# Softmax shifts and residuals of the last units, moved from GpSimd to VectorE

## The chip, the cores and the metric

The kernel runs on one core of one Trainium2 chip. A core has five engines with a queue of instructions each: TensorE (PE in the profile, its weight loads PEld), VectorE (DVE), ScalarE (ACT), GpSimd (POOL) and SyncE (SP), which here only issues DMAs. An engine takes its instructions in the order in which they are written; engines wait for each other by semaphores. The metric is the device time of one execution in microseconds (us). The kernel before takes 2047.81 us, the median of four runs.

## The reference, cut to what matters

Four graph layers work on `x`, 32 graphs of 512 nodes with 64 features, and share one adjacency matrix of 512 x 512. Each layer first normalizes its input and applies a relu, and its result is added to its input. Layers 0 to 2 are done before the part that this document is on. Layer 3 is graph attention with eight heads of width 128, and then one more attention to bring the result back to 64 features:

```python
def gat_layer(x, graph, W, b):
    h = x @ W
    s = jnp.einsum('bnd,bmd->bnm', h, h) * graph
    s = jnp.where(s == 0.0, NEG_INF, s)
    a = jax.nn.softmax(s, axis=2)
    return jnp.einsum('bnm,bmd->bnd', a, h) + b
heads = jax.vmap(lambda W, b: gat_layer(flow_x, graph, W, b))(Wh, bh)
x = jax.nn.leaky_relu(cat, negative_slope=0.01)
out = gat_layer(x, graph, W_out, b_out)
return jax.nn.leaky_relu(out, negative_slope=0.01)
# layer 3 of the stack: x = x + that
```

A softmax subtracts the largest score of a row before the exponential. The kernel has this subtraction as an operation of its own, called `shift`. The last sum, `x +`, is called the residual.

## The kernel before, in words

Layer 3 is cut into 144 units. A unit is a pair of attention matrices of 512 x 512: two graphs of one pair of heads (`Heads`, 128 units), or the second attention of two graphs (`Out`, 16 units). The list `flow` holds them in order; the last eight of the list are all `Out` units. In this document units are numbered from 0, so the last is 143. The function `period(t)` (L737) is called for t from -10 to 149 and writes out, in a fixed order, one step for each of several units that are at different stages: `unit(lag)` is unit t - lag, or nothing where there is none. TensorE, VectorE, ScalarE, GpSimd and SyncE all keep the order written there.

The scores of a unit are kept in four row blocks r = 0 to 3 of 128 rows, each a tile `p_att` of 128 x 1024 numbers of 4 bytes for the two matrices. Around the change, a unit u goes through these steps; the period in which it does is given as u + lag:

- lag 0: `scores` (L383, TensorE) and `maxima` (L395, VectorE) make each block and its largest values; `spread_out` and `spread_in` (L402, L410, SyncE) send these out and bring them back as a broadcast tile `topb` by DMA.
- lag 1: `shift(r, engine)` (L414 to L420) subtracts `topb` from block r. It is one operation of 128 x 1024 (L416), but two halves of 128 x 512 for r = 0 (L420). `exps(r)` (L429, ScalarE) takes the exponential, for r = 1 and 3 into PSUM (`e_ps`); `join(r)` (L432, VectorE) adds block r and block r - 1. `make_v` (L629 to L633) makes the right-hand sides.
- lag 2: `totals` (L450, TensorE, L456, ScalarE) and `totals_out` (L461, DMA to `parts`) make the sums of rows, `values` (L438, TensorE) the product with the features, `recips` (L467, L470, VectorE) the reciprocals, which `recips_out` (L474) sends out.
- lag 3: `recips_in` (L481) brings the reciprocals back as a broadcast tile `recb`, and `normalize` (L487, VectorE) multiplies by it.
- lag 4, `Out` units: `bias` (L660, ScalarE), `back` (L670 transposes on TensorE, L675 on ScalarE) and `back_dve` (L678, VectorE, the leaky relu).
- lag 5, `Out` units: `back_pool` (L684) adds the residual, in two operations of 128 x 256, one for each graph.
- lag 6, `Out` units: `store` (L691, SyncE), one DMA for each graph.

In every period but t = 1 all four shifts are GpSimd's. In t = 1, when nothing else runs yet, they are VectorE's, in the order 0, 2, 1, 3, at one place of the period: behind `normalize` of lag 3 and the maxima, and ahead of `back`, `back_dve`, `values`, `recips` and `join`. The residuals are all GpSimd's. At t = 145 `any_zero` (L695 to L720) works out a flag, which every engine reads at the end (L1839) to skip a general form of the kernel that isn't needed with these inputs.

Of the kernel before, what the change touches and what calls it, by code (L numbers as in the profile page):

```python
# [22 lines left out]
def fast_form(  # L23
# [25 lines left out]
    nc = tc.nc  # L49
# [276 lines left out]
    class Pair:  # L326
# [42 lines left out]
        def back_dve(self):  # L369
            pass  # L370

        def back_pool(self):
            pass

        def store(self):
# [224 lines left out]
    class Out(Pair):  # L600
# [78 lines left out]
                self.y, self.ps, -1.0, self.w, op0=OP.add, op1=OP.max  # L679
            )  # L680

        def back_pool(self):
            for k in range(2):
                nc.gpsimd.tensor_tensor(  # L684
                    self.y[:, :, k], self.y[:, :, k],
                    xs[self.b // G][:, self.b % G + k], OP.add,
                )
# [7 lines left out]
    def any_zero():  # L695

        def across(src, rows, name):
            ps = ps_m.tile([P, P], F32, name=name, tag="m")
            n = src.shape[0]
            nc.tensor.transpose(ps[:rows, :n], src, ident[:n, :n])  # L700
            return ps[:rows, :n]

        own = tiny.tile([P, 1], F32, name="own")
        nc.vector.tensor_reduce(own, least, AX.X, OP.min)
        two = tiny.tile([1, 2], F32, name="two")
        nc.vector.tensor_reduce(two[:, 0:1], across(own, 1, "own_ps"), AX.X, OP.min)
        best = tiny.tile([B // 2, 2], F32, name="best")
        nc.vector.tensor_reduce(
            best,
            across(least_out, B // 2, "out_ps").rearrange("b (k f) -> b k f", k=2),  # L710
            AX.X, OP.max,
        )
        worst = tiny.tile([B // 2, 1], F32, name="worst")
        nc.vector.tensor_reduce(worst, best, AX.X, OP.min)
        nc.vector.tensor_reduce(
            two[:, 1:2], across(worst, 1, "worst_ps"), AX.X, OP.min
        )
        flag = tiny.tile([1, 1], F32, name="flag")
        nc.vector.tensor_reduce(flag, two, AX.X, OP.min)
        nc.vector.scalar_tensor_tensor(  # L720
            again, flag, 0.0, unsound, op0=OP.is_equal, op1=OP.max
        )
# [6 lines left out]
    def planned(units, products):  # L729

        class Nothing:
            def __getattr__(self, name):
                return lambda *args: None

        nothing = Nothing()

        def period(t):  # L737
            def unit(lag):
                return units[t - lag] if 0 <= t - lag < len(units) else nothing

            now, ahead = unit(0), unit(-1)
            for r in range(2, C):
                now.scores(r)
            unit(3).recips_in()
            unit(6).store()
            unit(4).bias()
            if t != 1:
                unit(1).shift(0, nc.gpsimd)
                unit(1).exps(0)
            unit(2).totals()  # L750
            unit(2).totals_out(1, nc.scalar)
            u, h = products.get(t - 1, (None, 0))
            if u and h == H - 1:
                u.keep_product()
            if t != 1:
                unit(1).shift(2, nc.gpsimd)
                unit(1).exps(2)
            for r in range(2, C):
                now.maxima(r)
            now.spread_out()  # L760
            unit(2).totals_out(0, nc.sync)
            now.spread_in()
            for r in range(2):
                ahead.scores(r)
            unit(4).y_pe()
            unit(4).y_act()
            unit(3).normalize()
            for r in range(2):
                ahead.maxima(r)
            if t == 1:  # L770
                for r in (0, 2, 1, 3):
                    unit(1).shift(r, nc.vector)
                    if r < 3:
                        unit(1).exps(r)
            unit(4).back()
            unit(4).y_dve()
            unit(4).back_dve()
            if t != 1:
                unit(1).shift(1, nc.gpsimd)
                unit(1).exps(1)  # L780
            for j in range(C):
                unit(2).values(j)
            u, h = products.get(t, (None, 0))
            if u:
                u.product(h)
            unit(2).recips()
            unit(2).recips_out()
            unit(1).join(1)
            if t != 1:
                unit(1).shift(3, nc.gpsimd)  # L790
            unit(1).exps(3)
            unit(5).back_pool()
            unit(-2).make_gs()
            unit(1).join(3)
            unit(-3).features(3)
            unit(-2).judge_product()
            unit(1).make_v()
            unit(-4).make_hx()
            unit(-2).make_g()
            for step in range(3):  # L800
                for lag, odd in ((step - 7, 0), (step - 11, 1)):
                    u = unit(lag)
                    if getattr(u, "i", None) == 0 and u.b % 2 == odd:
                        u.features(step)
            if t == len(units) + 1:
                any_zero()

        return period
# [1067 lines left out]
```

## Time and profile before

| | us |
|---|---|
| median of four runs (2045.85 to 2050.99) | 2047.81 |
| the profiled execution's own time | 2049.11 |
| its span, from the first to the last instruction | 2047.2 |
| TensorE busy in the span | 1981.7 (97%) |
| VectorE busy | 1752.8 (86%) |
| GpSimd busy | 1444.8 (71%) |
| ScalarE busy | 1296.2 (63%) |
| GpSimd's shifts, 128 x 1024 (L416): 429 of them, mean 2.377 | 1007.0 |
| GpSimd's shifts, halves of r = 0 (L420): 286 of them, mean 1.278 (busy) | 359.7 |

A line of a timeline reads: start in us from the span's start, length, engine, line of the kernel, operation, what is written and read, how many, and in brackets how long the engine stood idle before and who ended that. In a line of a chain of waits the start is followed by the length and by the engine and line that the end had to wait for then. Where one source line is asked for, the three numbers behind the count are the shortest, the median and the longest duration in ns, followed by the first and last start in us.

### The profile page before, as it was taken

The page shows a single profiled execution, that of the slowest core. Times are in us where ns is not written, and L with a number is a line of the kernel's source. Part 1 is how long each engine was busy: PE and PEld are TensorE (multiplying, and loading weights), DVE is VectorE, ACT ScalarE, POOL GpSimd, SP SyncE. Part 2 cuts the span into 40 slices and gives each one's busy share as a digit, 9 for nine tenths or more (in the row PEclk, how much of TensorE's full clock was granted, in tenths as well). Part 3 has the DMA queues.
Part 4 walks back from the last instruction along what each step waited for, and adds up shares of the span by engine and source line. Part 5 has one row for each costly group of instructions (what it writes and reads, how often), then busy time and mean ns, then how long its engine had stood idle before and what let it go on. Part 6 is the DMA issues. An engine that isn't in the chain of part 4 may idle for free.

```text
span 2047.2 us, 32571 instructions
## 1 busy us (share of the span) xinstructions
PE 1981.7 (97%) x11038; PEld 812.4 (40%) x11038; DVE 1752.8 (86%) x4121; ACT 1296.2 (63%) x1960; POOL 1444.8 (71%) x834
## 2 busy tenths in 40 slices
PE   7999999997999999999999999999999999999995
PEld 4676676762333333333333333333333333333332
DVE  6699996768888889889889988988888898888994
ACT  3443443346677777767677777676676776766674
POOL 2000000006898989899988999898898988989996
PEclk9999999988999999999999999999999999999998
DMA  5000000002222323333332323332333332333233
GB/s 143 1 1 1 1 2 1 2 1 69 74 69 79 84 75 76 78 81 78 75 84 74 84 69 84 74 77 77 74 77 72 79 72 72 79 74 78 71 84 80
DMA packets 186464, 129.31 MB, mean 63 GB/s; under 512 B 125048, under 2 KB 130336, under 8 KB 186160
## 3 DMA queue, kind: packets, MB, share of 16 engines
q1 hardware_dynamic: 167056, 126.35, 24.3%
q10 hardware_dynamic: 18720, 0.59, 0.5%
q8 instruction: 89, 1.46, 0.3%
q14 instruction: 87, 0.71, 0.1%
q0 software_dynamic: 512, 0.20, 0.1%
HBM read 119.48 MB, written 5.37 MB: 61 GB/s over the span
## 4 chain that ended last, share of the span: by engine, by line
PE 57%; POOL 6%; DVE 5%; DMA 4%; ACT 3%; issue 2%; ACTq 0%; SPq 0%; POOLq 0%; DVEq 0%
PE s_ps L383 20%; PE av L438 19%; PE tot_ps L450 5%; POOL p_att L416 5%; PE y_ps L568 5%; PE gT_ps L613 4%; PE g_ps L550 3%; DVE p_att L395 2%; DVE p_att L432 1%; POOL p_att L420 1%; DMA recb<-rec_row 1%; DMA topb<-top_row 1%; DVE cat L586 1%; DMA top_row<-top 1%; DMA rec_row<-rec_flow 1%
## 5 line engine op out<-in xcount | busy, mean ns | idle before, releaser
L416 POOL TENSOR_TENSOR p_att<-p_att,topb 128x1024 f32<-128x1024 f32 x429 | 1007.0, 2377 | 0.0
L395 DVE CUSTOM_DVE_ANT_0 p_att<-s_ps,flow_neg 128x512 f32<-128x512 f32 x1152 | 726.1, 686 | 88.5 <-PE s_ps L383 87.1
L383 PE MATMUL s_ps<-g,hx 64*128 64x512 f32 x2048 | 516.2, 614 | 18.2 <-DVE p_att L432 16.1
L420 POOL TENSOR_TENSOR p_att<-p_att,topb 128x512 f32<-128x512 f32 x286 | 359.7, 1278 | 174.3 <-DMA topb<-top_row 143.2
L429 ACT ACTIVATE p_att<-p_att 128x1024 f32<-128x1024 f32 x288 | 304.8, 1059 | 174.9 <-POOL p_att L420 92.0
L432 DVE TENSOR_TENSOR p_att<-e_ps,p_att 128x1024 f32<-128x1024 f32 x288 | 338.6, 1198 | 34.8 <-ACT e_ps L429 33.8
L429 ACT ACTIVATE e_ps<-p_att 128x1024 f32<-128x1024 f32 x288 | 293.3, 1029 | 91.2 <-POOL p_att L416 79.4
L383 PEld LDWEIGHTS s_ps<-g,hx 64*128 64x128 f32 x2048 | 174.7, 186 | 331.5 <-DVE top L395 173.0
L438 PE MATMUL av<-p_att,hd 128*64 128x512 f32 x1024 | 269.8, 605 | 0.7 <-DVE o_att L487 0.6
L438 PE MATMUL av<-p_att,hn 128*64 128x512 f32 x1024 | 263.5, 592 | 0.0
L1090 POOL TENSOR_TENSOR x<-x,bias_b 128x512 f32<-128x512 f32 x16 | 20.3, 1274 | 280.9 <-DVE hn L863 280.9
L586 DVE SCALAR_TENSOR_TENSOR cat<-y_ps,bh,cat 128x512 f32<-128x512 f32 x256 | 180.0, 745 | 15.1 <-ACT cat L578 14.0
L562 ACT COPY g<-g_ps 128x512 f32<-128x512 f32 x128 | 132.0, 1139 | 80.1 <-PE g_ps L550 80.0
L578 ACT ACTIVATE cat<-y_ps,bh 128x512 f32<-128x512 f32 x256 | 161.2, 681 | 32.5 <-PE y_ps L568 31.5
L450 PE MATMUL tot_ps<-p_att,ones 128*32 128x512 f32 x1152 | 156.0, 607 | 4.3 <-DVE p_att L432 4.3
L568 PE MATMUL y_ps<-o_att,wh_sb 64*128 64x512 f32 x512 | 137.5, 594 | 0.0
L438 PEld LDWEIGHTS av<-p_att,hn 128*64 128x64 f32 x1024 | 74.2, 137 | 145.5 <-issue 145.5
L613 PE MATMUL gT_ps<-cat,wo_sb 128*64 128x512 f32 x512 | 131.7, 592 | 0.0
L487 DVE TENSOR_TENSOR o_att<-av,recb 128x512 f32<-128x512 f32 x144 | 99.2, 689 | 35.8 <-DMA recb<-rec_row 34.7
L438 PEld LDWEIGHTS av<-p_att,hd 128*64 128x64 f32 x1024 | 62.6, 136 | 166.0 <-issue 138.9
L1014 PE MATMUL acc<-v,s 64*128 64x65 f32 x2048 | 124.1, 280 | 0.7 <-DVE s L1000 0.4
L1014 PEld LDWEIGHTS acc<-v,s 64*128 64x128 f32 x2048 | 121.1, 195 | 5.9 <-DVE o L1030 1.2
(183 smaller groups left out, 2113.2 us busy)
## 6 DMA issues: line engine op xcount, KB each, us to landing
topb<-top_row SPq DMA_DIRECT2D x288, 256.0 KB
recb<-rec_row SPq DMA_DIRECT2D x288, 128.0 KB
out_dram<-y SPq DMA_DIRECT2D x32, 128.0 KB
x<-in_x_dram SPq DMA_DIRECT2D x3, 1024.0 KB
top_row<-top SPq DMA_DIRECT2D x144, 4.0 KB
parts<-tot SPq DMA_DIRECT2D x144, 4.0 KB
parts<-tot ACTq DMA_DIRECT2D x144, 4.0 KB
rec_row<-rec_flow SPq DMA_DIRECT2D x144, 4.0 KB
```

Of the source, the lines that this page charges most:

```text
L383: nc.tensor.matmul(ps[:, k], lhsT=x[halves(k), r * P : (r + 1) * P], rhs=g[halves(k), :], start=True, stop=True,)
L395: nc.vector.tensor_tensor_reduce(out=self.p[r][:, k], in0=ps[:, k], in1=flow_neg[:, r], scale=-1.0, scalar=BIG, op0=OP.add, op1=OP.min, ac ...
L416: engine.tensor_tensor(self.p[r], self.p[r], self.topb, OP.subtract)
L420: engine.tensor_tensor(p, p, self.topb[:, k], OP.subtract)
L429: nc.scalar.activation(to, self.p[r], AF.Exp, scale=-1.0)
L432: nc.vector.tensor_tensor(self.p[r], self.joined, self.p[r - 1], OP.add)
L438: nc.tensor.matmul(self.av[halves(k), :], lhsT=self.v(k, j) if j % 2 else self.less_next(k, j), rhs=self.p[j][:, k], start=(j == 0), stop= ...
L450: nc.tensor.matmul(ps[q : q + 32, :], lhsT=ones, rhs=self.p[2 * e + 1][:, k], start=True, stop=True,)
L568: nc.tensor.matmul(ps, lhsT=wh_sb[halves(k), 2 * self.i + k, :], rhs=self.o[halves(k), :], start=True, stop=True,)
L586: nc.vector.scalar_tensor_tensor(self.cat[:, k], self.y[k], bh[:, h : h + 1], self.cat[:, k], op0=OP.add, op1=OP.max,)
L613: nc.tensor.matmul(self.gps[halves(k), :], lhsT=wo_sb[:, h, :], rhs=Heads.cat.pop((self.b + k, h)), start=(h == 0), stop=(h == H - 1),)
L1014: nc.tensor.matmul(self.acc[k][:, r], lhsT=self.s[b // 2][halves(k), b % 2, r * P : (r + 1) * P], rhs=self.v[halves(k), b], start=(b == 0) ...
```

## The change: what it does

A tuple `quick` now says which shifts of the period are VectorE's: all four in t = 1, as before, and in t = 144, where the last unit is at lag 1; blocks 1 and 3 in t = 143, for the last unit but one; none elsewhere. They stand where the shifts of t = 1 stood. The residual (`back_pool`, now `residual`) takes its engine as an argument: GpSimd up to t = 146, VectorE in t = 147 and 148, which are those of units 142 and 143. Its place in the period stays, behind `exps(3)` and so behind `back_dve` of the next unit.

```diff
-        def back_pool(self):
+        def residual(self, engine):
             for k in range(2):
-                nc.gpsimd.tensor_tensor(
+                engine.tensor_tensor(
                     self.y[:, :, k], self.y[:, :, k],
                     xs[self.b // G][:, self.b % G + k], OP.add,
                 )
...
+            end = len(units)
             now, ahead = unit(0), unit(-1)
+            quick = (0, 2, 1, 3) if t in (1, end) else (1, 3) if t == end - 1 else ()
...
-            if t != 1:
+            if 0 not in quick:
                 unit(1).shift(0, nc.gpsimd)
                 unit(1).exps(0)
...
-            if t != 1:
+            if 2 not in quick:
                 unit(1).shift(2, nc.gpsimd)
                 unit(1).exps(2)
...
-            if t == 1:
-                for r in (0, 2, 1, 3):
-                    unit(1).shift(r, nc.vector)
-                    if r < 3:
-                        unit(1).exps(r)
+            for r in quick:
+                unit(1).shift(r, nc.vector)
+                if r < 3:
+                    unit(1).exps(r)
             unit(4).back()
             unit(4).y_dve()
             unit(4).back_dve()
-            if t != 1:
+            if 1 not in quick:
                 unit(1).shift(1, nc.gpsimd)
                 unit(1).exps(1)
...
-            if t != 1:
+            if 3 not in quick:
                 unit(1).shift(3, nc.gpsimd)
             unit(1).exps(3)
-            unit(5).back_pool()
+            unit(5).residual(nc.gpsimd if t < end + 3 else nc.vector)
             unit(-2).make_gs()
             unit(1).join(3)
```

## The prediction

> **What bounds the kernel now.** I read the page first: span 2047.2 us, PE busy 97%. The change touches the last units of 144, so the page as a whole says nothing on it. What counts is the last 45 us, so I read the chain of waits there (start, length, what), in order of time:
>
> ```profile
> 2013.72 2.49 POOL p_att L420 x2
> 2016.22 4.64 POOL p_att L416 x2
> ...
> 2020.88 1.04 ACT e_ps L429
> ...
> 2021.94 1.24 DVE p_att L432
> ...
> 2023.20 1.04 ACT e_ps L429
> ...
> 2024.26 1.24 DVE p_att L432
> ...
> 2027.25 2.27 DMA parts<-tot
> ...
> 2030.04 1.39 DMA rec_row<-rec_flow
> ...
> 2039.71 0.51 POOL y L684
> ```
>
> GpSimd's subtractions (L420, L416) of the last unit, call it 143, end the wait of its exponentials; then two additions (L432), sums, a round trip of DMAs for the reciprocals, the normalization, and GpSimd's residual. The stretches named by POOL are what the change takes away: period 143 starts at 2002.92 with unit 142's subtractions, period 144 at 2013.72 with unit 143's.
>
> Next the timeline of VectorE in period 144, because its queue receives the work (start, length, operation, idle before it and who ended that):
>
> ```profile
> 2014.63 0.41 DVE L633 TENSOR_TENSOR gD<-gV_ps,gV 128x256 f32<-128x256 f32 x1
> 2016.84 0.69 DVE L487 TENSOR_TENSOR o_att<-av,recb 128x512 f32<-128x512 f32 x1 [1.80 <-DMA recb<-rec_row]
> 2020.13 0.69 DVE L678 SCALAR_TENSOR_TENSOR y<-back_ps,y 128x512 f32<-128x512 f32 x1 [2.60 <-ACT y L675]
> 2020.74 0.16 DVE L467 TENSOR_REDUCE rec_flow<-parts 128x8 f32<-128x16 f32 x1
> ```
>
> See the second row: the normalization of unit 141 (L487) waits for a DMA until 2016.84. In the changed kernel unit 143's four subtractions stand behind it in VectorE's queue. GpSimd started them 3.1 us earlier, at 2013.72.
>
> Last, SyncE's stores at the end:
>
> ```profile
> 2037.32 1.22 SPq L691 DMA_DIRECT2D out_dram<-y  x2
> 2040.46 0.53 SPq L691 DMA_DIRECT2D out_dram<-y  x1
> 2041.14 0.54 SPq L691 DMA_DIRECT2D out_dram<-y  x1
> ```
>
> Unit 142's two stores leave at 2037.32, unit 143's at 2040.46 and 2041.14, each as soon as GpSimd has made its half. The span ends 6.10 us after the last one starts.
>
> **The change part by part.** Prices of the operation on VectorE, from the first unit, where it already does this, and on GpSimd:
>
> ```profile
> L416 POOL TENSOR_TENSOR p_att<-p_att,topb x429: 2342/2377/2424, 475.8 to 2020.8; 128x1024 f32<-128x1024 f32 x143
> L416 DVE TENSOR_TENSOR p_att<-p_att,topb x3: 1215/1218/1219, 470.0 to 472.3; 128x1024 f32<-128x1024 f32 x3
> L420 POOL TENSOR_TENSOR p_att<-p_att,topb x286: 1257/1274/2062, 472.6 to 2015.0; 128x512 f32<-128x512 f32 x143
> L420 DVE TENSOR_TENSOR p_att<-p_att,topb x2: 684/686/687, 468.8 to 469.4; 128x512 f32<-128x512 f32 x2
> ```
>
> VectorE needs 1.22 us for what takes GpSimd 2.38. Back to back they started 1.15 us apart, the halves (L420) 0.60 apart. ScalarE starts its next operation 0.1 us before the last one's end; a hop between engines is 0.03 us.
>
> *Period 143* (unit 142: two subtractions go to VectorE). GpSimd still does r=0 and r=2, until 2007.76. VectorE ends unit 140's normalization at 2007.59 and does r=1 and r=3. GpSimd goes on from 2007.73 with unit 138's residual, two times 0.72. In this period alone both engines work at two SBUF operands side by side. The only row of that case is the 2062 in the L420 line: GpSimd's half took 0.79 more than its median while VectorE's last L416 ran beside it. So for VectorE's wait I take a turn each: r=1 from 2007.76 to 2008.98, r=3 behind one residual half, 2009.6 to 2010.8. Bounds: no wait at all (r=3 ends at 2009.9), or both halves first (r=3 ends at 2011.5). Behind r=3 in the queue stand L678 of unit 139 (to 2011.4), and the reciprocals of unit 141, whose row then leaves on SyncE's queue at 2011.8 instead of 2010.40. That DMA landed at 2013.31, 0.17 behind the broadcast (`topb`) issued before it, while the same row takes 1.39 to 1.41 us where nothing is ahead of it (2030.04, 2021.17). 2011.8 and 1.4 make 2013.2: still hidden under the broadcast. With both halves first it leaves at 2013.0, lands at 2014.4, and costs 1.1 us. Below nothing is excluded: it can't land ahead of the packets before it. I take 0. Unit 142's totals come some 0.7 us sooner, and are not waited for: its reciprocals stand behind period 144's work on VectorE.
>
> *Period 144* (unit 143: all four to VectorE). Normalization of unit 141 at 2016.84 as before, then from 2017.44 the two halves, 18.66 r=2, 19.80 r=1, 20.95 to 22.17 r=3. ScalarE's exponential of r=1 starts at 2021.05, where it had started at 2020.88: GpSimd's 9.5 us became 4.7, started 3.7 later, with r=1 third in both orders. Now ScalarE has L675 of unit 140 after this exponential instead of before it: 2021.98 to 2022.57. VectorE follows with L678 (2022.60), the two reciprocal instructions (2023.21), and the first L432 at 2023.53, where before it started at 2021.94. r=3's exponential is done by 2023.5, so the second L432 runs from 2024.62 to 2025.84; before it ended at 2025.50 (2024.26 and 1.24). **Cost: +0.35 us.** The same queue delays unit 142's reciprocals from 2020.74 to 2023.2, so its normalization goes from 2026.45 to about 2028.9. What is late next is PE's values of unit 143 behind it (3.66 us, now to 2033.3) and the end flag's chain (1.75 us, now to 2035.0). Unit 143's own reciprocals need the normalization and L678 of unit 141 done, 2030.0, against 2029.61: 0.39 with the +0.35 in it. Its broadcast then ends at 2035.4, so the two late chains stay just covered, by 0.4 us. On SyncE's queue the broadcast of unit 142's reciprocals goes from 2022.58 to 2025.05, and the two stores of unit 139 behind it end at 2027.6, where unit 143's partial sums (`parts`) are wanted at 2027.61 and are to land at 2029.9: covered, with nothing to spare. GpSimd's residuals of units 139 to 141 wait only for their own L678 and for no one.
>
> *Residuals of units 142 and 143.* GpSimd made them in two times 0.70 (2039.71 to 2041.11). On VectorE a 128x256 sum takes 0.41 (the L633 row), 0.34 apart. But in the written order unit 142's residual stands one period after its L678, and so behind unit 143's L678 in VectorE's queue. That L678 started at 2038.89 and now starts at 2039.28. Unit 142's two sums run 2039.88 to 2040.64, instead of 2036.57 to 2037.98 in GpSimd's free time, and unit 143's end at 2041.32. Sums alone are a wash: +0.2 against 2041.11. The stores are not: all four are now queued on SyncE from 2040.33, 0.68 apart (2037.32 and 2038.00 in the trace), so the last starts at 2040.33 + 3 x 0.685 = 2042.38 instead of 2041.14. **Sum: +1.24 us**, of it 0.39 by the late chain and 0.85 by the stores.
>
> *After the last store.* Of its 16 parts, 14 had landed 2.24 us after it started and the last one after 4.30; in the trace's DMA rows a 16 KB fetch of instructions runs from 2043.34 to 2044.44. VectorE and GpSimd reach the flag's branch at other times in the changed kernel, so this can fall away: then the end hangs on SyncE's own last waits, at 2046.8 against 2047.24 (-0.5 in all). Or it falls on more stores. I keep the 4.30, as the stores' parts are on the rings for longer than before.
>
> So the span goes from 2047.24 to 2048.5. The profiled execution took 2049.11, 1.3 over the median of 2047.81 of the four runs; the same difference on the median gives **2049.1 us**, 0.06% more. 0.2% (4.1 us) is about what a measurement of this kernel can tell from no change.
>
> One rule stands against the change. The Trainium skill, page "SBUF — State Buffer", section "SBUF: two separate sides", says that a VectorE operation with two SBUF inputs and a GpSimd operation that reads SBUF hold one port pair in turn, whole instructions long, whichever came first. The row shows GpSimd as the loser, once; none shows VectorE losing. By the row alone VectorE waits for nothing, by the rule up to both residual halves; the sum is +1.2 or up to +2.3.
>
> **Rivals.**
> - *GpSimd was the bound and the gain arrives.* If unit 143's subtractions start when their broadcast has landed (2013.2) and nothing stands in front, the last L432 ends at about 2021.5, 4.0 sooner, and with 0.7 off the residual the time is 2043.1. For it: the chain names POOL from 1985.93 to 2020.86 almost without a break. Against it: L487 in front, whose DMA SyncE issues only at 2013.32. It decides only if that broadcast lands before 2013.2, which the queue forbids.
> - *The stores escape the fetch*: -0.5, 2047.3. For it: normal landings of 2.3 us; against: three of the last four stores had a part 1.4 us or more behind the rest.
> - *VectorE loses the port to both halves*: +1.1 more, 2050.1. For it: GpSimd is ready 0.03 us after its own last operation. Against: VectorE has waited since 2007.5.
> - *Slower beyond doubt: the end's fetches fall on the bunched stores.* Place: the landing of the last store; price 2.06 us for each hit (4.30 less 2.24). It decides from two further hits: +1.2 + 4.1, 2053.1. For it: four stores on the rings at once; against: only a hit on the last counts in full.
>
> **How the numbers follow.** Forecast as worked out 0.55, escape 0.22, lost port 0.12, bunched fetches 0.07, full gain 0.04. Faster takes only the full gain, 0.04; slower only the fetches, 0.07; the rest, 0.89, is within 0.2%. The range runs from the escape to the lost port, 2047.3 to 2050.1, widened by 1.9 us at both ends, the distance of the lowest run from the median: 2045.4 to 2052.0.
>
> **What would show it.** Right: L487 of unit 141 still near 2016.84 with the subtractions behind it; the last L432 ending within 0.5 of 2025.8; four stores 0.68 apart at the end. Wrong: L416 on VectorE over 1.3 us, L487 later than 2017.5, or a first L432 of unit 143 before 2023. The prediction fails if that normalization comes earlier, or if the last store's landing changes by more than 2 us.

## The result, and the profile after

The changed kernel takes 2051.79 us (median of 41 runs, 2048.05 to 2056.78), the kernel before, run beside it, 2048.9 us (63 runs, 2045.74 to 2053.73). The ratio is 1.0014 with a 95% interval of 1.0009 to 1.0018, so the change costs 2.9 us (1.8 to 3.7). The profiled execution took 2051.79 us, with a span of 2050.0. Two kernels of the study were also profiled a second time under a name of their own (E11 and E13 below), so each has two tails.

I measure the tail from the start of unit 140's normalization (L487 in period 143) to the end of the span. In front of that point the traces drift against each other whatever the kernel: the normalization starts at 2006.90 and 2009.06 in the two profiles of the kernel before, and at 2008.23 and 2008.32 in those of the changed kernel. The tail, cut at points that both kernels have (us):

| stretch | before, twice | changed, twice | mean difference |
|---|---|---|---|
| unit 140's L487 to unit 141's L487 | 9.94, 10.01 | 10.69, 10.73 | +0.74 |
| to the end of unit 143's last join (L432) | 8.64, 8.30 | 9.00, 9.00 | +0.53 |
| to the copy of the totals (L456) | 1.15, 2.02 | 2.02, 1.15 | 0 |
| to unit 143's L487 | 8.51, 8.89 | 8.40, 8.62 | -0.19 |
| to unit 143's L678 | 3.74, 3.74 | 3.33, 3.33 | -0.41 |
| to the start of the last store | 2.25, 2.25 | 3.06, 3.05 | +0.81 |
| to the landing of the last store | 4.30, 4.05 | 3.49, 3.60 | -0.63 |
| to the end | 1.80, 1.80 | 1.79, 1.79 | 0 |
| whole tail | 40.34, 41.07 | 41.77, 41.27 | +0.82 |

The chain of waits of the changed kernel, in order of time (start, length, what the end had to wait for):

```profile
2008.84 2.56 DVE p_att L416
...
2011.41 1.03 ACT e_ps L429
...
2012.44 0.53 ACT y L675
...
2014.02 1.39 DMA rec_row<-rec_flow
...
2019.61 1.20 DVE p_att L420 x2
2020.81 2.28 DVE p_att L416 x2
...
2025.70 1.10 DVE p_att L432
...
2026.93 2.98 PE tot_ps L450 x8
...
2042.36 0.34 DVE y L684
```

Where the chain of before named GpSimd for the last subtractions and the residual, it now names VectorE, and the last join comes later for it: it ends 19.69 us after the start of unit 140's normalization instead of 18.59. Its first line is new: one L416 of unit 142 on VectorE, 2.54 us long (2.56 with what follows it in the chain). Behind it the chain goes over ScalarE's exponential (L429) and L675 to unit 141's reciprocals. VectorE's and GpSimd's timelines around it (start, length, engine, line, operation, count):

```profile
2006.52 2.41 POOL L416 TENSOR_TENSOR p_att<-p_att,topb 128x1024 f32<-128x1024 f32 x1
2008.23 0.69 DVE L487 TENSOR_TENSOR o_att<-av,recb 128x512 f32<-128x512 f32 x1 [0.38 <-ACT tot L456]
2008.84 3.68 DVE L416 TENSOR_TENSOR p_att<-p_att,topb 128x1024 f32<-128x1024 f32 x2
2008.84 1.45 POOL L684 TENSOR_TENSOR y<-y,x 128x256 f32<-128x256 f32 x2
```

Two subtractions of 1.22 us each took 3.68 together, while GpSimd's residual of unit 138 ran in two halves from 2008.84 to 2010.29. Asked for by source line, L416 shows that the case stands alone (shortest, median and longest in ns, first and last start in us):

```profile
L416 DVE TENSOR_TENSOR p_att<-p_att,topb x8: 1212/1218/2543, 470.6 to 2023.0; 128x1024 f32<-128x1024 f32 x8
```

Period 144 on VectorE in the same kernel:

```profile
2018.92 0.69 DVE L487 TENSOR_TENSOR o_att<-av,recb 128x512 f32<-128x512 f32 x1 [2.37 <-DMA recb<-rec_row]
2019.53 1.28 DVE L420 TENSOR_TENSOR p_att<-p_att,topb 128x512 f32<-128x512 f32 x2
2020.73 3.49 DVE L416 TENSOR_TENSOR p_att<-p_att,topb 128x1024 f32<-128x1024 f32 x3
...
2025.61 2.31 DVE L432 TENSOR_TENSOR p_att<-e_ps,p_att 128x1024 f32<-128x1024 f32 x2
```

The normalization of unit 141 waits for its DMA as before, and the subtractions stand behind it. From its start to the end of the second L432 are 9.00 us. SyncE's last stores:

```profile
2042.71 0.53 SPq L691 DMA_DIRECT2D out_dram<-y  x1
2043.30 0.63 SPq L691 DMA_DIRECT2D out_dram<-y  x1
2044.02 0.60 SPq L691 DMA_DIRECT2D out_dram<-y  x1
2044.72 0.59 SPq L691 DMA_DIRECT2D out_dram<-y  x1
```

All four of units 142 and 143 leave in one row, about 0.7 us apart, where before, unit 142's had left 3.1 us ahead.

### The profile page after: what moved, and what is told of

It reads as the page before. It is cut to its first block, busy times and chain, and to the rows that moved or that the text cites. A ratio compares the mean times of both kernels' runs of the same rounds, so it can differ in the third digit from the quotient of the medians.

```text
span 2050.0 us, 32562 instructions
## 1 busy us (share of the span) xinstructions
PE 1984.6 (97%) x11038; PEld 813.4 (40%) x11038; DVE 1763.0 (86%) x4132; ACT 1295.4 (63%) x1960; POOL 1429.0 (70%) x823
## 4 chain that ended last, share of the span: by engine, by line
PE 58%; POOL 6%; DVE 5%; DMA 4%; ACT 2%; issue 1%; SPq 0%; ACTq 0%; DVEq 0%; POOLq 0%
PE s_ps L383 20%; PE av L438 19%; PE tot_ps L450 5%; POOL p_att L416 5%; PE y_ps L568 5%; PE gT_ps L613 4%; PE g_ps L550 3%; DVE p_att L395 2%; DMA topb<-top_row 2%; DVE p_att L432 1%; POOL p_att L420 1%; ACT e_ps L429 1%; PE hx_ps L310 1%; DMA rec_row<-rec_flow 1%; DMA top_row<-top 1%
## 5 line engine op out<-in xcount | busy, mean ns | idle before, releaser
L416 POOL TENSOR_TENSOR p_att<-p_att,topb 128x1024 f32<-128x1024 f32 x424 | 996.4, 2383 | 0.0
L429 ACT ACTIVATE p_att<-p_att 128x1024 f32<-128x1024 f32 x288 | 304.7, 1058 | 179.4 <-POOL p_att L420 92.8
L432 DVE TENSOR_TENSOR p_att<-e_ps,p_att 128x1024 f32<-128x1024 f32 x288 | 338.9, 1197 | 34.0 <-ACT e_ps L429 32.6
L429 ACT ACTIVATE e_ps<-p_att 128x1024 f32<-128x1024 f32 x288 | 293.3, 1029 | 93.5 <-POOL p_att L416 85.1
L450 PE MATMUL tot_ps<-p_att,ones 128*32 128x512 f32 x1152 | 156.9, 609 | 4.9 <-DVE p_att L432 4.9
L487 DVE TENSOR_TENSOR o_att<-av,recb 128x512 f32<-128x512 f32 x144 | 99.2, 689 | 37.0 <-DMA recb<-rec_row 35.1
```

The costliest lines, as they stand in the source:

```text
L416: engine.tensor_tensor(self.p[r], self.p[r], self.topb, OP.subtract)
L429: nc.scalar.activation(to, self.p[r], AF.Exp, scale=-1.0)
L432: nc.vector.tensor_tensor(self.p[r], self.joined, self.p[r - 1], OP.add)
L450: nc.tensor.matmul(ps[q : q + 32, :], lhsT=ones, rhs=self.p[2 * e + 1][:, k], start=True, stop=True,)
```

## The experiments

The theory after the result was a sum of separate costs: VectorE waits for the SBUF port beside GpSimd's residual (+0.75), the last joins come later (+0.35 to +0.7), unit 142's stores fill SyncE's queue in front of unit 143's (+0.8), and TensorE's clock comes and goes. The rival was that the changed queues as a whole cost this time and no part by itself. All ratios are to the kernel before on the same chip in the same series. Times in the table are us, with the cuts of the table above.

| run | ratio, 95% interval | L487 of 140 to 141 | to last join's end | to totals copied | L678 to last store | last store's landing | tail |
|---|---|---|---|---|---|---|---|
| E1 shifts only | 1.0005, 0.9996 to 1.0014 | 11.12 | 9.00 | 1.15 | 2.50 | 4.12 | 42.52 |
| E2 residuals only | 1.0002, 0.9993 to 1.0011 | 9.86 | 8.45 | 1.69 | 3.05 | 3.21 | 40.14 |
| E3 last unit's shifts only | 1.0006, 0.9997 to 1.0015 | 9.59 | 9.00 | 2.02 | 2.20 | 2.40 | 39.58 |
| E4 unit 138's residual moved | 1.0009, 1.0000 to 1.0018 | 9.95 | 8.99 | 1.91 | 3.05 | 3.12 | 40.95 |
| E5 early shifts, last residual | 1.0003, 0.9994 to 1.0012 | 12.76 | 4.10 | 4.17 | 1.80 | 2.54 | 39.48 |
| E6 early shifts | 1.0008, 0.9999 to 1.0017 | 12.72 | 4.09 | 4.01 | 2.20 | 4.05 | 41.07 |
| E7 fill | 1.0011, 1.0002 to 1.0020 | 10.77 | 9.00 | 3.13 | 3.06 | 3.78 | 43.68 |
| E9 split | 0.9988, 0.9976 to 1.0001 | 9.81 | 7.79 | 1.15 | 2.04 | 2.59 | 38.09 |
| E10 one residual | 0.9999, 0.9988 to 1.0010 | 11.07 | 9.00 | 1.15 | 1.81 | 2.57 | 40.31 |
| E11 changed, again | 1.0012, 1.0002 to 1.0021 | 10.73 | 9.00 | 1.15 | 3.05 | 3.60 | 41.27 |
| E12 split, reciprocals first | 0.9987, 0.9978 to 0.9995 | 9.95 | 7.52 | 1.15 | 1.80 | 2.73 | 37.49 |
| E13 before, again | 0.9997, 0.9988 to 1.0006 | 10.01 | 8.30 | 2.02 | 2.25 | 4.05 | 41.07 |

### E1, E2 and E3: the change in parts

E1 leaves the shifts moved and gives the residuals back to GpSimd:

```diff
-            unit(5).residual(nc.gpsimd if t < end + 3 else nc.vector)
+            unit(5).residual(nc.gpsimd)
```

> The changed shifts of units 142 and 143, with all residuals on GpSimd again. Measure: the tail from the start of unit 140's normalization (L487, period 143) to the end of the span; 40.34 us in the kernel before, 41.77 in the changed one. Theory A (the sum of the prediction, with the sizes read from the changed kernel's trace: port +0.75, late join +0.35, TensorE at half clock +0.87, stores +0.81): without the stores' part the last store starts 2.25 us after unit 143's L678, as before, instead of 3.06, and the tail is 40.9 to 41.8, depending on the landing of the last store. Rival B (the loss is the residuals' alone): tail 40.3, time as before. Against the kernel before: A +0.05 to +0.12%, B 0.

E2 moves the residuals and leaves the shifts as before:

```diff
-            quick = (0, 2, 1, 3) if t in (1, end) else (1, 3) if t == end - 1 else ()
+            quick = (0, 2, 1, 3) if t == 1 else ()
```

> Only the residuals of units 142 and 143 are VectorE's; all shifts but the first unit's are GpSimd's. Theory A: everything up to unit 143's L678 as before, last store 3.06 instead of 2.25 us after it, tail 40.34 + 0.81 less what the landing of the last store gives back (0 to 2.06): 39.1 to 41.2. Rival B (the loss is the residuals' alone): the whole loss, +0.09 to +0.18%. Rival C (the loss is the shifts' alone): tail 40.3 and no change.

E3 moves only the shifts of unit 143, not the two of unit 142, and no residual:

```diff
-            quick = (0, 2, 1, 3) if t in (1, end) else (1, 3) if t == end - 1 else ()
+            quick = (0, 2, 1, 3) if t in (1, end) else ()
...
-            unit(5).residual(nc.gpsimd if t < end + 3 else nc.vector)
+            unit(5).residual(nc.gpsimd)
```

> Unit 143's four shifts on VectorE, unit 142's all on GpSimd, residuals on GpSimd. Theory A (the 0.75 us between the normalizations of units 140 and 141 come from unit 142's two shifts, which wait for GpSimd's port and so hold back unit 141's reciprocals): that stretch is 9.9 again, instead of 10.7; from unit 141's normalization to the end of the last join 9.0, as in the changed kernel; against the kernel before +0.02 to +0.06%. Rival D (the stretch of 10.7 is a slower DMA or chance): it stays at 10.7.

The terms go with their parts. The longer first stretch is there in E1 (11.12), where unit 142's shifts are moved, and not in E2 and E3 (9.86, 9.59). The 9.00 us to the last join's end are there in E1 and E3, and not in E2 (8.45). The 3.05 us from L678 to the last store are in E2 alone (2.50 and 2.20 in the others). Timed one by one, none of the three can be told from the kernel before: each interval holds 1.

E1's tail, 42.52, is longer than the 40.9 to 41.8 that were expected, because of a cost that the changed kernel doesn't pay in its two profiles. Its chain of waits:

```profile
2027.57 0.70 DVE o_att L487
...
2028.32 5.35 PE av L438 x16
2033.67 0.21 PE own_ps L700
...
2033.91 0.28 DVE two L706
...
2035.31 0.70 DVE o_att L487
```

TensorE ran unit 143's `values` at half its clock, 5.35 us where 3.65 is usual, and the end flag's instructions, which stand on VectorE ahead of unit 143's normalization, waited for it. The stretch from the totals to that normalization became 9.51 us instead of 8.5. The cover that I had put at 0.4 us is as thin as that.

### E4: take the port collision away

E4 is the changed kernel with unit 138's residual on VectorE too, in period 143, where VectorE makes it after its own subtractions. GpSimd then has nothing to do beside them:

```diff
-            unit(5).residual(nc.gpsimd if t < end + 3 else nc.vector)
+            unit(5).residual(nc.gpsimd if t < end + 3 and t != end - 1 else nc.vector)
```

> The changed kernel, and unit 138's residual in period 143 is VectorE's too, so that GpSimd has no work beside unit 142's second shift on VectorE. Theory A (port): VectorE's shift of block 1 takes 1.2 to 1.5 us instead of 2.55, block 3 1.2, and unit 141's normalization comes 9.9 to 10.1 after unit 140's instead of 10.7; tail 0.6 to 0.75 shorter than the changed kernel's. Rival D: no change in that stretch, 10.7, and L416 still takes 2.5.

VectorE's timeline of E4 at the same place:

```profile
2009.88 0.69 DVE L487 TENSOR_TENSOR o_att<-av,recb 128x512 f32<-128x512 f32 x1 [0.29 <-DMA recb<-rec_row]
2010.49 2.40 DVE L416 TENSOR_TENSOR p_att<-p_att,topb 128x1024 f32<-128x1024 f32 x2
```

The two subtractions take 2.40 us instead of 3.68, and the stretch to unit 141's normalization is 9.95 again, as in the kernel before. So GpSimd's residual beside the subtractions made the 0.75: the two subtractions take 1.28 us longer with it, and 0.74 of that reaches unit 141's normalization, whose reciprocals stand behind them on VectorE and behind L675 on ScalarE. On the clock of whole runs the step is too small to see: E4's ratio, 1.0009 (1.0000 to 1.0018), can't be told from the changed kernel's 1.0014.

VectorE didn't get in between the halves in any of the five profiles with that neighbourhood (changed, E1, E7, E10, E11). In E1 its operation is even recorded as starting ahead of the first half, while GpSimd's subtraction of block 2 was still running (to 2005.40):

```profile
2002.94 2.46 POOL L416 TENSOR_TENSOR p_att<-p_att,topb 128x1024 f32<-128x1024 f32 x1
2005.13 3.87 DVE L416 TENSOR_TENSOR p_att<-p_att,topb 128x1024 f32<-128x1024 f32 x2
2005.27 1.50 POOL L684 TENSOR_TENSOR y<-y,x 128x256 f32<-128x256 f32 x2
```

VectorE's first subtraction ended at 2007.86, 1.08 us after GpSimd's second half, and so it did in the other four. In E4, where no half followed, it ended 1.08 us after GpSimd's subtraction of block 2 (2011.75 and 2010.67). The Trainium skill, page "SBUF — State Buffer", section "SBUF: two separate sides", says that the two engines share a pair of ports by a lock: whichever instruction starts first holds it to its end, and the other engine is blocked. That VectorE is shut out altogether agrees with 2.44 to 2.73 us in the five profiles against 1.21 to 1.26 in E4. Whether the first to start wins can't be read from these records: in four of the five VectorE's operation is recorded as starting before GpSimd's subtraction of block 2 had ended, and each of GpSimd's three operations starts 0.03 to 0.13 us before the one ahead of it ends, so the ports may never have been free between them. What they show is that GpSimd made both its halves first each time.

### E10: what holds the last stores

E10 is the changed kernel with unit 142's residual back on GpSimd:

```diff
-            unit(5).residual(nc.gpsimd if t < end + 3 else nc.vector)
+            unit(5).residual(nc.gpsimd if t < end + 4 else nc.vector)
```

> The changed kernel with unit 142's residual back on GpSimd; unit 143's stays on VectorE. Theory (SP's queue is filled by unit 142's two stores just ahead): from unit 140's normalization to unit 141's 10.7 and from there to the end of the last join 9.0, as in the changed kernel; from L678 of unit 143 to the start of the last store 1.75 instead of 3.06; the tail 1.3 us shorter than the changed kernel's at the same landing, 39.4 to 41.3. Rival (the stores are held by something else): 2.25 or more.

SyncE's timeline of E10 has two stores at the end where the changed kernel has four:

```profile
2044.12 1.22 SPq L691 DMA_DIRECT2D out_dram<-y  x2
```

From L678 to the last store's start are 1.81 us instead of 3.06, as expected: unit 142's stores in front made the wait, and VectorE's faster sums by themselves are a gain of 0.44 against the 2.25 of before. Its ratio is 0.9999 (0.9988 to 1.0010), though unit 142's shifts still pay for the port (11.07).

### E7, E11 and E13: TensorE's clock

In the first profile of the changed kernel the sums of rows (L450) ran at half clock, which took 0.87 us more than in the first profile of before. E7 tries to keep TensorE busy in front of them with five matrix products whose result nobody reads:

```diff
             unit(1).make_v()
+            if t == end:
+                p = ps_g.tile([P, N], F32, name="gT_ps")
+                for i in range(5):
+                    nc.tensor.matmul(p, lhsT=ident, rhs=urow, start=True, stop=True)
```

> The changed kernel with five matmuls of 128x128 by 128x512 more on TensorE (their product is not used), behind unit 143's gV in period 144, where TensorE otherwise stood idle for 2.9 us before the last sums of rows. Theory A (the half clock comes from that idle time): the clock stays full up to these sums, ScalarE's copy of them starts 1.15 us after the last join ends instead of 2.02, and the tail is 0.9 shorter than the changed kernel's 41.77, at equal landing of the last store. Rival F (the clock falls at times of its own): the clock is granted at half in 2024 to 2031 again and the copy starts 1.7 to 2.0 after the join.

This one missed its aim. The trace has ten records for the five products, 4.46 us, and the sums had to wait for them, 3.13 us from the join to the copy. The sums behind the fill did run at full clock, but the price of the half clock couldn't be read from it.

E11 is the changed kernel once more, with nothing edited, and E13 the kernel before once more.

> The changed kernel itself, for a second profile of its tail. Port theory: from unit 140's normalization to unit 141's 10.7 us again, with one L416 on VectorE of 2.5 or more beside GpSimd's residual; 9.0 from there to the end of the last join; 3.06 from L678 to the last store's start; tail 40.7 to 42.5. If the half clock comes from TensorE's idle time in front of the last sums, it falls there again (2.0 us from the last join's end to the copy of the totals). Rival (it falls where it falls, by the run): 1.15 there, and the tail 0.9 shorter at the same landing.

> The kernel before, once more under a name of its own, for a second profile of its tail and for the size of a difference between two series of the same kernel. If the half clock in the tail belongs to the run and not to the changed queues, it can fall in this tail too, and the stretch from unit 140's normalization to the last store's start is 34.2 us (as before) plus what the half clock adds to TensorE's part; the landing of the last store lies anywhere from 2.4 to 4.3. Ratio 0.9993 to 1.0007. If the landing of 4.30 belongs to this kernel, it is 4.0 or more again.

In E11 the port and the stores came out as in the first profile (10.73, 9.00, 3.05), and the sums ran at full clock (1.15). In E13, the kernel before, they ran at half clock (2.02). So the 0.87 comes and goes with the run, in both kernels. Where it falls can be read from windows of 3.41 us, the length of a stretch at half clock, laid on its edges (window, length, then busy time and count of PE, PEld, DVE, ACT and POOL, and then the clock). First the kernel before, in its first profile:

```profile
2020.06:2023.48 3.42, 2.02 (x12) 0.76 (x10) 2.20 (x4) 1.35 (x3) 3.42 (x3) 1.00 0.02 1
2023.48:2026.89 3.41, 2.24 (x11) 0.51 (x8) 1.99 (x3) 2.62 (x4) 2.44 (x4) 1.00 0.65 154
2026.89:2030.30 3.41, 3.29 (x17) 1.31 (x17) 1.47 (x5) 2.03 (x3) 0.96 (x2) 1.00 0.07 7
```

The same kernel in E13:

```profile
2023.98:2027.39 3.41, 1.22 (x6) 0.17 (x4) 2.32 (x3) 2.31 (x3) 3.41 (x5) 1.00 0.32 87
2027.39:2030.80 3.41, 3.38 (x10) 1.20 (x12) 1.00 (x2) 1.08 (x3) 0.41 (x1) 0.50 0.29 67
```

The changed kernel in its first profile:

```profile
2024.14:2027.55 3.41, 0.62 (x4) 0.17 (x4) 2.90 (x6) 3.04 (x5) 1.42 (x2) 1.00 0.02 1
2027.55:2030.96 3.41, 3.39 (x11) 0.90 (x8) 0.79 (x3) 0.59 (x1) 0.00 (x0) 0.50 0.54 152
```

And in E11:

```profile
2017.44:2020.85 3.41, 1.42 (x10) 0.69 (x10) 1.80 (x3) 0.50 (x1) 0.00 (x0) 1.00 0.52 129
2020.85:2024.26 3.41, 3.41 (x12) 1.20 (x10) 3.41 (x4) 3.13 (x4) 0.00 (x0) 0.50 0.00 0
```

Of the windows shown, those in which PE was busy for 1.42 us or less are followed by one at half clock, and behind those of 2.02 us and more the clock is full. The same holds for the 236 such windows of all fourteen profiles from 1990 us on: behind the 58 in which TensorE was busy for 0.45 of the time or less the clock was at half, behind the 169 with 0.54 or more it was full, and behind the nine between it was at half four times. The grid of these windows lies differently in each run, so the same idle time falls into one window in one run and into two in the next. The Trainium skill, page "TensorE: Matmul & The Clock Gate", Part 1, has a free-running window of 3413 ns, which agrees with the 3.41; it speaks of an idle window, while here one that was 0.42 busy was enough. Whether the changed kernel falls into half clock more often, because its idle time ahead of the sums is in one piece (2.94 us in its first profile; 1.40 and 1.17 apart in the first profile of before), can't be told from two profiles each.

### E5 and E6: the subtractions ahead of the normalization

The prediction's rival of a full gain needed that nothing stands in front of unit 143's shifts on VectorE. E6 puts them ahead of unit 141's normalization and takes back the rest of the change; E5 also leaves unit 143's residual on VectorE:

```diff
-            quick = (0, 2, 1, 3) if t in (1, end) else (1, 3) if t == end - 1 else ()
+            quick = (0, 2, 1, 3) if t in (1, end) else ()
...
+            def quicken():
+                for r in quick:
+                    unit(1).shift(r, nc.vector)
+                    if r < 3:
+                        unit(1).exps(r)
+            if t == end:
+                quicken()
             unit(3).normalize()
...
-            for r in quick:
-                unit(1).shift(r, nc.vector)
-                if r < 3:
-                    unit(1).exps(r)
+            if t != end:
+                quicken()
```

> Unit 143's four shifts on VectorE, but ahead of unit 141's normalization in its queue; unit 142's shifts and all residuals on GpSimd. Theory A (the queue position is what eats the gain): the shifts start when unit 142's last addition is done, the last join ends 16.6 us after unit 140's normalization starts (18.59 in the kernel before, 19.69 in the changed one), unit 141's normalization comes at 12.9 instead of 9.9, and unit 142's still at 19.7. Tail 38.4 with TensorE at full clock in the last values, up to 39.9 at half clock. Rival E (VectorE's shifts gain nothing at the end whatever their place, since the DMA round trips set it): last join earlier, but tail 40.3 and no change in time.

> As the early shifts, and unit 143's residual alone on VectorE, unit 142's left to GpSimd. Theory A: the two last stores are then not behind unit 142's; the last starts 1.7 us after unit 143's L678, instead of 2.25 in the kernel before and 3.06 in the changed one. Tail 37.9 to 39.4, less or more by the landing of the last store; against the kernel before -0.05 to -0.12%. Rival E: last store 2.25 or more after L678, no change in time.

The joins did come sooner: the last one ended 16.82 us after unit 140's normalization in E6 and 16.85 in E5, against 18.59 and 18.31 before. The totals didn't. TensorE's timeline of E6:

```profile
2021.73 1.97 PE L438 MATMUL av<-p_att,gD 128*64 128x512 f32 x4 [4.05 <-DVE o_att L487]
2023.46 1.73 PE L438 MATMUL av<-p_att,gV 128*64 128x512 f32 x4
2025.01 1.04 PE L438 MATMUL av<-p_att,gD 128*64 128x512 f32 x4
2025.87 1.04 PE L438 MATMUL av<-p_att,gV 128*64 128x512 f32 x4
...
2027.43 1.06 PE L450 MATMUL tot_ps<-p_att,ones 128*32 128x512 f32 x8
```

Unit 141's normalization came 2.7 us later than before, unit 142's `values` waited 4.05 us for it, because there is one accumulator `av`, and then took 5.18 us instead of 3.65, the first half of them at half clock. The sums are behind them in TensorE's queue and started 2.4 us after the last join had ended (2024.99). What was won on VectorE was lost on TensorE, and the expected tails (38.4 to 39.9 us in E6, 37.9 to 39.4 in E5) were missed: 41.07 and 39.48.

### E9 and E12: a version that is faster

E9 splits the difference: shift 0 of unit 143, the two halves of 0.6 us, goes ahead of unit 141's normalization, into time in which VectorE waits for that DMA anyway, and shifts 2, 1 and 3 behind it. Unit 142's shifts and residual are GpSimd's again, so there is no port collision and no extra store in the queue; unit 143's residual stays on VectorE.

```diff
-            quick = (0, 2, 1, 3) if t in (1, end) else (1, 3) if t == end - 1 else ()
+            quick = (0, 2, 1, 3) if t in (1, end) else ()
...
+            if t == end:
+                unit(1).shift(0, nc.vector)
+                unit(1).exps(0)
             unit(3).normalize()
...
             for r in quick:
+                if t == end and r == 0:
+                    continue
...
-            unit(5).residual(nc.gpsimd if t < end + 3 else nc.vector)
+            unit(5).residual(nc.gpsimd if t < end + 4 else nc.vector)
```

> Unit 143's shift 0 is subtracted on VectorE ahead of unit 141's normalization, its shifts 2, 1 and 3 behind it; unit 142's shifts and residual go back to GpSimd, and only unit 143's residual is on VectorE. Theory (the tail is a sum of separate terms: port, joins, store queue): from unit 140's normalization to unit 141's about 9.9 us (10.69 in the changed kernel, 9.94 before); last join ends about 17.8 after unit 140's normalization (18.59 before, 19.69 changed); from L678 of unit 143 to the start of the last store about 1.75 (2.25 before, 3.06 changed); the tail from unit 140's normalization to the end about 39.2 at the landing of before, 0.02 to 0.08% under the kernel before. Rival (TensorE takes it back, as in e6 and e5: values or sums late or at half clock): the totals start no sooner than before and the tail is 40.3 or more.

The join came 17.60 us after unit 140's normalization, a little better than expected, the last store later than expected (2.04 instead of 1.75), and the tail was 38.09. But 9.57 us went by between the totals and unit 143's normalization, the flag's chain again: unit 143's `values` ran at half clock, as in E1. One line of E9's chain of waits:

```profile
2029.81 5.35 PE av L438 x16
```

E12 adds to E9 that unit 142's reciprocals and the DMA of their row go ahead of shift 3:

```diff
+                if t == end and r == 3:
+                    unit(2).recips()
+                    unit(2).recips_out()
                 unit(1).shift(r, nc.vector)
...
-            unit(2).recips()
-            unit(2).recips_out()
+            if t != end:
+                unit(2).recips()
+                unit(2).recips_out()
             unit(1).join(1)
```

> The split order of e9, with unit 142's reciprocals and the DMA of their row ahead of unit 143's shift 3 on VectorE instead of behind it and behind L678 of unit 140. In e9 the last stretch, from the copy of the totals to the normalization of unit 143, was 9.57 us instead of 8.5, because unit 142's normalization came at 20.6 after unit 140's and unit 143's values and the flag's chain stood behind it. Theory: the reciprocals leave 2.2 us sooner; unit 142's normalization comes 18.4 to 18.8 after unit 140's, the last join ends 17.3 (0.3 sooner than e9), and the last stretch is 8.4 to 8.6 again; tail 36.5 to 37.5 at e9's landing of 2.59 (40.34 in the kernel before, of it 1.7 by its longer landing); ratio to the kernel before 0.998 to 0.9995. Rival (something else holds unit 143's normalization): the last stretch stays over 9.2 and the tail at 37.8 or more.

VectorE's timeline of E12:

```profile
2014.70 1.35 DVE L420 TENSOR_TENSOR p_att<-p_att,topb 128x512 f32<-128x512 f32 x2
2016.85 0.69 DVE L487 TENSOR_TENSOR o_att<-av,recb 128x512 f32<-128x512 f32 x1 [0.80 <-DMA recb<-rec_row]
2017.46 2.35 DVE L416 TENSOR_TENSOR p_att<-p_att,topb 128x1024 f32<-128x1024 f32 x2
2019.72 0.17 DVE L467 TENSOR_REDUCE rec_flow<-parts 128x8 f32<-128x16 f32 x1
2019.92 0.20 DVE L470 RECIPROCAL rec_flow<-rec_flow 128x8 f32<-128x8 f32 x1
2020.04 1.17 DVE L416 TENSOR_TENSOR p_att<-p_att,topb 128x1024 f32<-128x1024 f32 x1
...
2022.03 2.35 DVE L432 TENSOR_TENSOR p_att<-e_ps,p_att 128x1024 f32<-128x1024 f32 x2
```

Unit 142's normalization now starts 18.15 us after unit 140's (20.60 in E9), the stretch to unit 143's is 8.74, and the tail is 37.49 us against 40.34 and 41.07 before. Of the 3.2 us against their mean, 1.0 is the earlier join (17.47 against 18.45), 0.45 the earlier last store (1.80 against 2.25), 1.45 the landing (2.73 against 4.18), for which no cause is shown; the rest lies with the clock. E12 takes 2047.16 us against 2049.6 us for the kernel before beside it, a ratio of 0.9987 (0.9978 to 0.9995): 0.13% faster than the kernel before, and faster than the changed kernel too, whose ratios are 1.0014 and 1.0012. What the earlier reciprocals add to E9 isn't shown: E12's `values` ran at full clock (3.65 us), which alone could make the 0.6 us between the two tails, and the two ratios, 0.9988 and 0.9987, are the same.

## Why the prediction was right or wrong

The time came out as forecast in kind: within 0.2% and on the slower side, with 2051.79 inside the range, though at its upper end. In that there is luck: without the 1.9 us by which the range was widened for the scatter of single runs it would end at 2050.1. Nor is 0.2% what a measurement of this kernel can tell; this one told 0.14% from no change. The predicted median of 2049.1 is 2.7 us too low; 1.1 of that is the base, as four runs had put the kernel before at 2047.81 and 63 runs put it at 2048.9. The rest is the size of the change: +1.24 predicted, +2.9 (1.8 to 3.7) measured in the first series, +2.5 (0.4 to 4.3) in E11's.

- **Period 143, "a turn each", cost 0: wrong.** VectorE waited for both halves, the case that I had as a rival at 1.1 us with a chance of 0.12. The step that failed is the choice between the bounds: one row had GpSimd as the loser, and VectorE's long wait was to speak for it. The sign named for it, an L416 on VectorE over 1.3 us, is in the profile with 2.54. The mechanism of the rival was right: GpSimd had its next operation ready each time. It measured +0.75 where the rival had 1.1 (E4 takes it away, E1, E10 and E11 have it).
- **Period 144, 9.00 us from unit 141's L487 to the end of the last L432: right.** It is 9.00 in the profile after, and in each kernel with unit 143's four shifts behind that normalization. As a cost, +0.35, it is +0.36 against the first profile of before and +0.70 against the second.
- **The two late chains, covered by 0.4: right, and as thin as said.** In the profile after, unit 143's normalization waited for its broadcast, not for the flag; in E11 the chain of waits runs through the flag, at a cost of 0.1 to 0.2, and in E1 through the slow `values`, at 1.0.
- **Unit 142's normalization 2.45 later: right.** It is 3.1 later between the first two profiles (19.56 and 22.64 after unit 140's), 0.75 of it the port.
- **Stores, +0.85: right.** 3.06 us from L678 to the last store's start, where the working gave 3.10 and the kernel before has 2.25.
- **Landing of the last store, kept at 4.30: wrong in size.** It is 3.49 and 3.60, a gain of 0.63 on average, between the forecast and the rival of an escape. What sets it isn't shown.
- **TensorE's clock: missing from the sum.** It moved single stretches by -0.4 to +0.9, in both kernels, by the run.
- **The full gain: ruled out for the reason given.** Unit 141's normalization stands in front; and E6 shows that even ahead of it the gain stops at TensorE.

The terms that both profiles of each kernel share come to +1.4: joins +1.26, of it the port 0.74, stores +0.81, landing -0.63. That lies inside the interval of E11's series and 0.4 under the lower end of the first. What the remaining 0.4 to 2.3 us of the first series are stays open; a half clock that falls on the sums more often in the changed kernel would be a candidate, and no run here shows it.

## What to carry to other kernels

Before moving work from an engine that is the bound of a chain, see what the receiving engine's queue waits for just ahead of it: here 4.7 us on VectorE instead of 9.5 on GpSimd ended later, because the work stood behind a DMA wait. Put only the piece ahead of the wait that fits into it (E9, E12), and look for what the moved work pushes back on other queues: the next unit's reciprocals, the single accumulator, the stores. And where a VectorE operation with two SBUF inputs meets a GpSimd that is already at such work, count on VectorE waiting for all that GpSimd has ready, as in the five profiles here.

## What the runs showed that I had not expected

- GpSimd's two halves always went ahead of VectorE's operation, also where VectorE's is recorded 0.14 us earlier; GpSimd's subtraction ahead of them was then still running. GpSimd's own halves took 0.72 to 0.82 us there, as alone or up to 0.1 more.
- The landing of the last store goes with the engine of the last two residuals: 4.05 to 4.30 us with both on GpSimd (both profiles of before, E1, E6; but 2.40 in E3, where the end followed 2.66 us behind the landing instead of 1.8), 3.12 to 3.78 with both on VectorE (changed, E2, E4, E7, E11), 2.54 to 2.73 with only the last on VectorE (E5, E9, E10, E12). Of the store's 16 parts, one or two came 1.2 us or more behind the rest where it landed late (both profiles of before, first profile after), and none did in E3, E10 and E12. The fetches of instructions at the end could do that; it was not tried.
- One window of 3.41 us with TensorE busy for 0.45 of it or less put the next one at half clock each time; in E1 and E9 that made 5.35 us for `values` instead of 3.65.
